# Four graph layers on one core: pieces for the first adjacency, another queue for the weights, sums as a row, a last graph without collecting DMAs, and another planned order

## The chip, the cores and the metric

The kernel runs on one core of one Trainium2 chip, in fp32. The time is device microseconds of that core for one launch, as the median of several runs.

## What is computed

For each of 32 graphs of 512 nodes with 256 features there are four layers, each followed by a residual and a layer norm:

```python
x = layernorm(x + relu(((1 + eps) * x + adj @ x) @ W1 + b1) @ W2 + b2)  # 256 -> 512 -> 256
h = x @ W                                            # 4 heads of 64
e = where(adj > 0.5, leaky_relu(e_dst[i] + e_src[j], 0.2), -1e9)
x = layernorm(x + softmax(e) @ h + bias)             # each head
q, k, v = x @ Wq.T, x @ Wk.T, x @ Wv.T               # 8 heads of 32
s = q @ k.T / sqrt(32) + log(adj + 1e-6)
x = layernorm(x + (softmax(s) @ v) @ Wo.T + bo)
s = where(nodemask, adj * ((x @ W3) @ x.T), -1e30)
x = layernorm(x + softmax(s) @ x)
```

In the code the layers count from 0 to 3.

## The kernel before

**A plan sets the order.** `fast_path` does not write its instructions in order. It registers *steps* (`step(name, engine, us, after, take, free, mode)`), each with its engine, an assumed cost, the steps it comes after and the buffers that it takes and frees. `Plan.order` then runs a list scheduler over the steps of all graphs: among the steps that can start soonest it takes the one with the smallest due time, which is the graph's number times a period, less the longest path left, plus a random displacement of the step's name, plus a weight times the price of changing PE's form of matmul (`CHANGE`). `Plan.run` tries a few sets of parameters, keeps the one with the shortest planned end and emits the instructions in that order. Each engine works through its own in order, so the plan sets the order on every engine and on every queue of DMA issues. Several graphs are under way at a time, up to six (`live`), with 14 large buffers (`B`), 13 middle ones (`C`) and the 8 PSUM banks (`p`).

**Forms of matmul.** TensorE (PE) works in four forms, which the steps name by `mode`: the full array (""), four row tiles for layer 2's scores ("row", `32*128` in the profile), four column tiles of 32 for its values and weight sums ("c32", `128*32`), and two of 64 for layer 1's output ("c64", `128*64`).

**Set-up.** `prepare` loads the weights through `load` (L314 to 320, issue at L320), all on ScalarE's DMA queue: eps, w1 with b1, w2, three bias rows, wg with a0 and a1, rawq to rawo, w3. It transposes the layer-2 weights on PE (L341) and works out bounds (`gg`, L472; `fmt`, L493); a general path exists for inputs beyond them.

**One graph.** SyncE's queue (SP) loads x (L614) and then the adjacency A (L619), 0.5 and 1 MB.
- Layer 0: 16 PE transposes of A (`AT_t`, L639), copied by ScalarE to `AT` (L647); `hT_ps` = x times AT (L671); `h1T_ps` (L694), ScalarE's relu (L700); `y_ps` (L713). The layer norm takes DVE sums, a power on GpSimd (L577) and ScalarE's scaling (L590).
- Layer 1: transposes of x (ScalarE copies them and sums each row into `xs`); values `v1`; their logits. `R`, the exponentials of one side, is transposed on PE (`R_t`, L799), written to DRAM (`R_dram`) and read back to all partitions (`R_bc`), both on SP, L809 and 811. ScalarE and DVE build the weights z (L850, L861); `o_ps` (L884). Rows without an edge need a tiny share of the sum of all values: `hs` (step `hs`, L822) is that sum, Wg applied to `xs`, and `hse` (L830) scales it; `oe` adds it to the output as a per-partition bias.
- In layers 1 and 2 the softmax denominators are column sums of large weight tiles. Accumulating DMAs on GpSimd's queue add halves of the tiles together (L912 in layer 1, L1079 in layer 2: `collect`, steps `cd` and `cs`); PE then multiplies by ones (`d_ps`, step `d2` for layer 2, L1128), and DVE takes the reciprocal (L1143).
- Layer 2: transposes of x (`xT_t`, L990), q (`qT_ps`, L1009), k and v2; scores `s` (L1046), ScalarE's exp (L1059), DVE's product with adj (L1068), values (L1104), and the output projection `o2p_ps` (L1176) after DVE's product `yT` (L1147).
- Layer 3: A is loaded again; `iT_ps` (L1215), scores (L1229), ScalarE's exp (L1257), transposes (`eT_t`, L1274), output (L1301), and the store.

Of the kernel before, what the change touches and what calls it, by code (L numbers as in the profile page):

```python
# [30 lines left out]
def row_bcast(ap, n):  # L31

    return bass.AP(tensor=ap.tensor, offset=ap.offset, ap=[[0, P], [1, n]])
# [13 lines left out]
class Plan:  # L47
# [9 lines left out]
    BACK = {"act": 0.13, "dve": 0.12}  # L57

    CHANGE = {
# [4 lines left out]
    }  # L64
# [66 lines left out]
            t = max(t, ends[h][n] + self.hop(self.steps[h][n], s))  # L131
        return t

    def order(self, period, ahead, window, stay, shift=0.0, seed=0):
# [10 lines left out]
        rng = random.Random(seed)  # L145
        moved = {n: rng.uniform(-shift, shift) for n in [*self.steps[0], *self.steps[-1]]}

        def open_to(n):
            nonlocal opened
            while opened < min(n, len(self.steps)):  # L150
                for name in self.steps[opened]:
                    if not waits[opened][name]:
                        ready[opened, name] = self.ready(opened, name, ends)
                opened += 1

        open_to(window)
        while low < len(self.steps):
            found = []
            for (g, name), t in ready.items():
                s = self.steps[g][name]  # L160
                t = max(t, engine.get(s.eng, 0.0))
                change = self.CHANGE[mode][s.mode] if s.eng == "pe" else 0.0
                for k, (kind, _, rest) in enumerate(s.take):
                    r, n = room[kind], sum(b[0] == kind for b in s.take[:k])
                    if len(r) <= rest + n:
                        break
                    t = max(t, r[n][0])
                else:
                    due = max(g - 1, 0) * period - self.left[g][name] + moved[name] + stay * change
# [47 lines left out]
def fast_path(  # L217
# [77 lines left out]
    def prev(name, i):  # L295

        return (f"{name}{i-1}",) if i else ()
# [5 lines left out]
    def prepare():  # L303
# [7 lines left out]
        def bank(key, shape):  # L311
            return ps.tile(shape, F32, tag=f"p{slot[key]}", name=key)

        def load(name, us, *transfers, take=()):  # L314


            @step(f"ld_{name}", "act", 0.5 * len(transfers), take=take)
            def _():
                for transfer in transfers:
                    nc.scalar.dma_start(*transfer())  # L320

            @step(name, "q3", us, (f"ld_{name}",))
            def _():
                pass
# [25 lines left out]
            def _():  # L350
                nc.scalar.copy(wT[name].rearrange("p c f -> p (c f)"), t[f"wt{name}"])

        load("eps", 2.0, lambda: (eps_bc, row_bcast(eps0, 1)))
# [7 lines left out]
        load(  # L361
            "w1", 3.0, lambda: (w1_sb, rows(w1)), lambda: (b1_sb, b1.rearrange("(c p) -> p c", p=P))
        )
        load("w2", 2.5, lambda: (w2_sb, rows(w2)))

        def bias_rows(k, b):
# [5 lines left out]
        load("bias", 3.0, *(bias_rows(k, b) for k, b in enumerate((b2, gbias, bo))))  # L372

        def vector(name, a):
            def transfer():
# [2 lines left out]

            return transfer

        load(
            "wg", 3.0,
            lambda: (wg_sb[:, :, :D], wg.rearrange("(c p) h f -> p c (h f)", p=P)),
            vector("a0", a_src), vector("a1", a_dst), take=("C=a0", "C=a1"),
        )

        @step("wa", "dve", 3.2, ("wg",), take=("C=prod",), free=("prod", "a0", "a1"))
# [135 lines left out]
    def graph(g):  # L523
        plan.graph()
        slot = plan.slot[-1]
        t = {"g": g}

        def big(key, shape, name):
# [88 lines left out]
        def _():  # L617
            t["A"] = big("A0", [P, NC, N], "A")
            nc.sync.dma_start(t["A"], adj[g].rearrange("(c p) m -> p c m", p=P))  # L619

        @step("ld", "q0", 8.0, ("ldA",))
# [61 lines left out]
        for f in range(HC):  # L683

            @step(
                f"f{f}", "pe", 1.72, row("he", DC) + prev("f", f) + ("^w1",),
                take=(f"p=f{f}",) + (() if f else ("B=h1T/2",)),
            )
            def _(f=f):
# [124 lines left out]
        def _():  # L814
            pass

        @step("hs", "pe", 0.9, row("xe1", DC) + ("^wa",), take=("p=hs",))
        def _():
            ph = t["phs"] = bank("hs", [P, DC], "hs_ps")
            for o in range(DC):  # L820
                for d in range(DC):
                    nc.tensor.matmul(  # L822
                        ph[:, o : o + 1], wg_sb[:, d, blk(o)], t["xs"][:, d : d + 1],
                        start=(d == 0), stop=(d == DC - 1),
                    )

        @step("hse", "act", 0.1, ("hs",), free=("hs",))
        def _():
            t["hs"] = little([P, DC], "hs")
            nc.scalar.mul(t["hs"], t["phs"], TINY)  # L830

        for c in range(NC):

# [35 lines left out]
        for hp in range(H1 // 2):  # L869
            for k in range(2):  # L870
# [221 lines left out]
        def attend(k):  # L1092
# [14 lines left out]
                        start=(c == 0), stop=(c == NC - 1),  # L1107
                    )

            if c % 2:  # L1110
                collect(k, k - 1, (f"n{k-1}", f"m{k}1"))
            if c < NC - 1:
                return
# [5 lines left out]
                nc.scalar.copy(t["yT2"][:, o, :], t[f"n{o}"])  # L1119

            a = NC * o
            collect(a + 2, a, (f"cs{a+1}", f"cs{a+3}", f"n{a+2}"))

            @step(f"d2{o}", "pe", 0.87, (f"cs{a+2}",), take=(f"p=d2{o}",), free=(f"E{a}", f"zs{a}"), mode="c32")
            def _():
                t[f"d{o}"] = bank(f"d2{o}", [P, N], f"d2_ps_{o}")
                for j in range(4):
                    nc.tensor.matmul(  # L1128
                        t[f"d{o}"][32 * j : 32 * j + 32, :], ones[:, :32], t[f"E{a}"][:, j, :],
                        start=True, stop=True,  # L1130
                    )

            @step(f"nd{o}", "act", 0.49, (f"d2{o}",), take=(f"rdT=rdT{o}",), free=(f"d2{o}",))
            def _():
# [677 lines left out]
```

## Time and profile before

| | us |
|---|---|
| median of 3 runs (range) | 3014.66 (3010.17 to 3021.8) |
| profiled execution, time | 3013.04 |
| profiled execution, span | 3011.3 |
| PE busy | 2944.1 (98%) |
| DVE busy | 2009.7 (67%) |
| ScalarE (ACT) busy | 1946.5 (65%) |
| GpSimd (POOL) busy | 619.8 (21%) |
| mean granted TensorE clock | 0.991 of full speed |

The busy time of PE comes from ends that are modelled, so lengths on PE are read from start to start. Most fp32 matmuls leave two records in the trace, so eight records are four matmuls. In a line of the timeline stand the start, the length of the group, the engine, the source line, what it writes and reads, the count, and in brackets how long the engine was idle before it and what released it. A window's line has its length, then busy time and count for each engine, the granted clock, the share of DMA and its rate. A wait's line has the total, the number of times and the longest.

### The profile page before, as it was taken

How to read it: one execution, taken by the hardware profiler on the slowest of the kernel's cores; microseconds unless marked ns; L12 is line 12 of the kernel's file. 1: busy time of each engine (PE TensorE's matmuls, PEld its weight loads, DVE VectorE, ACT ScalarE, POOL GpSimd, SP SyncE). 2: the span in 40 equal slices, each digit the busy share in tenths (PEclk: the TensorE clock that was granted, in tenths of full speed). 3: DMA queues.
4: the chain of work that ended last, by engine and by line, in shares of the span. 5: the costliest groups of instructions: out<-in, count | busy, mean ns of one | idle time of the engine just before them, and what ended most of it. 6: DMA issues, size and time to landing. Idle time of an engine off the chain costs nothing. (4 is left out here: it accounts for less than half of the span.)

```text
span 3011.3 us, 40812 instructions
## 1 busy us (share of the span) xinstructions
PE 2944.1 (98%) x15053; PEld 1703.7 (57%) x15053; DVE 2009.7 (67%) x3935; ACT 1946.5 (65%) x3849; POOL 619.8 (21%) x686
## 2 busy tenths in 40 slices
PE   7899999999999999999999999999999999999996
PEld 5544655555565555565555565555565555565544
DVE  1467576676676676676676676676676676676874
ACT  2667566767666767666767666767666767666762
POOL 0222122112222112222112222112222112222210
PEclk9999999999999999999999999999999999999998
DMA  4579767788887788887787887787877787887963
GB/s 152 125 173 194 154 137 172 160 180 177 180 168 165 161 182 174 180 166 170 160 184 171 181 166 168 160 187 168 180 163 173 160 189 168 177 168 150 199 133 79
DMA packets 159782, 500.82 MB, mean 166 GB/s; under 512 B 13132, under 2 KB 48728, under 8 KB 130904
## 3 DMA queue, kind: packets, MB, share of 16 engines
q0 software_dynamic: 78336, 352.36, 62.0%
q1 hardware_dynamic: 77824, 142.88, 13.8%
q10 hardware_dynamic: 3416, 2.90, 0.3%
q8 instruction: 121, 1.98, 0.3%
q14 instruction: 85, 0.70, 0.1%
HBM read 179.06 MB, written 17.05 MB: 65 GB/s over the span
## 5 line engine op out<-in xcount | busy, mean ns | idle before, releaser
L1068 DVE SCALAR_TENSOR_TENSOR z<-AT,z 128x1024 f32<-128x1024 f32 x512 | 610.9, 1217 | 273.2 <-ACT z L1059 272.7
L1059 ACT ACTIVATE z<-s 128x512 f32<-128x512 f32 x1024 | 551.3, 611 | 268.3 <-PE s L1046 268.1
L1143 DVE RECIPROCAL rdT<-rdT 128x256 f32<-128x256 f32 x128 | 218.3, 1728 | 316.2 <-ACT rdT L1136 316.2
L861 DVE SCALAR_TENSOR_TENSOR z<-z,T,edge 128x512 f32<-128x512 f32 x512 | 357.8, 747 | 62.2 <-ACT z L850 62.0
L850 ACT ACTIVATE z<-R_bc,nT,S 128x512 f32<-128x512 f32 x512 | 382.1, 819 | 17.8 <-DMA R_bc<-R_dram 17.8
L1079 POOL DMA_DIRECT2D z<-z x192 | 169.5, 883 | 992.2 <-PE o_ps L1104 268.7
L590 ACT ACTIVATE x<-x,shift,rstd 128x256 f32<-128x256 f32 x512 | 295.4, 602 | 108.0 <-DVE shift L582 108.0
L912 POOL DMA_DIRECT2D z<-z x256 | 228.8, 1033 | 467.5 <-DMA z<-z 265.2
L1046 PE MATMUL s<-qT,kT 32*128 32x512 f32 x2048 | 291.8, 634 | 0.1
L577 POOL TENSOR_TENSOR rstd<-ve,nhalf 128x4 f32<-128x4 f32 x128 | 134.7, 1052 | 696.9 <-DVE ve L572 671.6
L1104 PE MATMUL o_ps<-z,v 128*32 128x512 f32 x2048 | 260.5, 601 | 0.3 <-ACT z L1059 0.3
L694 PE MATMUL h1T_ps<-hT,w_sb 128*128 128x512 f32 x512 | 240.0, 604 | 0.0
L1229 PE MATMUL s<-xT,iT 128*128 128x512 f32 x512 | 237.4, 598 | 0.0
L1301 PE MATMUL o_ps<-x,eT 128*128 128x256 f32 x1024 | 237.4, 385 | 0.0
L713 PE MATMUL y_ps<-w_sb,h1T 128*128 128x256 f32 x1024 | 232.4, 381 | 2.2 <-ACT h1T L700 2.2
L884 PE MATMUL o_ps<-z,v 128*64 128x512 f32 x1024 | 230.8, 602 | 1.5 <-DVE z L861 1.5
L1301 PEld LDWEIGHTS o_ps<-x,eT 128*128 128x128 f32 x1024 | 189.5, 190 | 68.1 <-issue 22.8
L713 PEld LDWEIGHTS y_ps<-w_sb,h1T 128*128 128x128 f32 x1024 | 194.6, 191 | 52.8 <-issue 20.7
L671 PE MATMUL hT_ps<-AT,x 128*128 128x384 f32 (+2 forms) x768 | 210.1, 383 | 8.8 <-ACT AT L647 8.8
L559 DVE BATCH_NORM_STATS2 st<-x 128x6 f32<-128x256 f32 x512 | 211.9, 414 | 5.6
L1046 PEld LDWEIGHTS s<-qT,kT 32*128 32x128 f32 x2048 | 93.5, 183 | 158.7 <-issue 66.8
L694 PEld LDWEIGHTS h1T_ps<-hT,w_sb 128*128 128x128 f32 x512 | 90.5, 190 | 122.0 <-issue 112.8
(145 smaller groups left out, 4261.5 us busy)
## 6 DMA issues: line engine op xcount, KB each, us to landing
z<-z POOLq DMA_DIRECT2D x192, 1024.0 KB, 8.2
A<-in_adj_dram SPq DMA_DIRECT2D x64, 1024.0 KB, 11.0
z<-z POOLq DMA_DIRECT2D x128, 512.0 KB, 8.0
x<-biases POOLq DMA_DIRECT2D x96, 512.0 KB, 9.6
R_bc<-R_dram SPq DMA_DIRECT2D x32, 1024.0 KB, 4.5
z<-z POOLq DMA_DIRECT2D x128, 256.0 KB, 7.7
x<-in_x_dram SPq DMA_DIRECT2D x32, 512.0 KB, 6.0
out_dram<-x SPq DMA_DIRECT2D x32, 512.0 KB, 3.8
```

The costliest lines, as they stand in the source:

```text
L590: nc.scalar.activation(t["x"][:, c, :], t["x"][:, c, :], AF.Identity, bias=t["shift"][:, c : c + 1], scale=t["rstd"][:, c : c + 1],)
L694: nc.tensor.matmul(ph, w1_sb[:, d, blk(f)], t["hT"][:, d, :], start=(d == 0), stop=(d == DC - 1))
L713: nc.tensor.matmul(py[:, j, :], t["h1T"][:, f, blk(2 * c2 + j)], w2_sb[:, f, :], start=(f == 0), stop=(f == HC - 1),)
L850: nc.scalar.activation(t[f"e{h}"][:, c, :], t["Rbc"][:, h, :], AF.Relu, bias=t["nT"][:, h, c : c + 1], scale=t["S"][:, h, c : c + 1],)
L861: nc.vector.scalar_tensor_tensor(z, z, t["T"][:, h, c : c + 1], t["edge"][:, c, :], op0=ALU.add, op1=ALU.mult)
L884: nc.tensor.matmul(po[j * F1 : (j + 1) * F1, :], t["v"][:, c, h * F1 : (h + 1) * F1], t[f"e{h}"][:, c, :], start=(c == 0), stop=(c == NC - 1),
L1046: nc.tensor.matmul(pk, t["k"][hs, o, blk(c)], t["q"][hs, o, :], start=True, stop=True)
L1059: nc.scalar.activation(t[f"E{k}"][:, j, :], t[f"ps{k}{j}"], AF.Exp, scale=QSCALE)
L1068: nc.vector.scalar_tensor_tensor(z, t["AT"][:, c, None, :].to_broadcast([P, 2, N]), ADJ_EPS, z, op0=ALU.add, op1=ALU.mult,)
L1104: nc.tensor.matmul(t[f"n{o}"][32 * j : 32 * j + 32, :], t["v2"][:, c, o * P + F2 * j : o * P + F2 * (j + 1)], t[f"E{k}"][:, j, :], start=( ...
L1229: nc.tensor.matmul(pt, t["iT"][:, d, blk(c)], t["xT3"][:, d, :], start=(d == 0), stop=(d == DC - 1),)
L1301: nc.tensor.matmul(py[:, j, :], t["eT"][:, m, blk(2 * c2 + j)], t["x"][:, m, :], start=(m == 0), stop=(m == NC - 1),)
```

## The change

The diff, cut to its core. It has six parts.

1. `CHANGE` prices the way from the full array to row tiles at 0.13 instead of 0.1, and back at 0.17 instead of 0.13.
2. `order` takes a list of (seed, size) pairs instead of one; each displaces a random 15% of the step names, and the displacements add up. One set of parameters with 14 such pairs takes the place of three.
3. `load` issues on SP. The small loads (eps, b1, the bias rows, a0 and a1) stay on ScalarE's queue, b1 apart from w1 and a0 and a1 apart from wg.
4. A is loaded ahead of x, for graph 0 in four pieces of columns, and the transposes of graph 0 wait for one piece each; `h` waits for x.
5. `hs` swaps weights and moving data: a row of 256 sums instead of two columns. The row goes to DRAM and back (on SP) to stand on the partitions; `oe` waits for that.
6. For the last graph nothing is collected by DMA; `d2` multiplies all four chunks of weights by ones and adds in PSUM.

```diff
-        "": {"": 0.0, "row": 0.1, "c32": 0.1, "c64": 0.1},
-        "row": {"": 0.13, "row": 0.1, "c32": 0.2, "c64": 0.2},
+        "": {"": 0.0, "row": 0.13, "c32": 0.1, "c64": 0.1},
+        "row": {"": 0.17, "row": 0.1, "c32": 0.2, "c64": 0.2},
...
-        moved = {n: rng.uniform(-shift, shift) for n in [*self.steps[0], *self.steps[-1]]}
+        moved = dict.fromkeys((n for steps in self.steps for n in steps), 0.0)
+        for seed, far in shifts:
+            rng = random.Random(seed)
+            for n in moved:
+                if rng.random() < 0.15:
+                    moved[n] += rng.uniform(-far, far)
...
-        def load(name, us, *transfers, take=()):
+        def load(name, us, *transfers, take=(), little=False):
-            @step(f"ld_{name}", "act", 0.5 * len(transfers), take=take)
+            @step(f"ld_{name}", "act" if little else "sp", 0.5 * len(transfers), take=take)
             def _():
                 for transfer in transfers:
-                    nc.scalar.dma_start(*transfer())
+                    (nc.scalar if little else nc.sync).dma_start(*transfer())
...
-        @step("ldx", "sp", 0.1, take=("live", "C=x/2"))
-        @step("ldA", "sp", 0.1, ("ldx",), take=("L0", "B=A0/5"))
+        pieces = NC if g == 0 else 1
+        for m in range(pieces):
+            @step(f"lp{m}", "sp", 0.4 if g == 0 else 0.1, prev("lp", m), ...)
+            def _(m=m):
+                cols = slice(m * N // pieces, (m + 1) * N // pieces)
+                nc.sync.dma_start(
+                    t["A"][:, :, cols], adj[g].rearrange("(c p) m -> p c m", p=P)[:, :, cols]
+                )
+        @step("ldx", "sp", 0.1, (f"lp{pieces-1}",), take=("C=x/2",))
...
-                f"at{m}", "pe", 0.44, ("ld",) + prev("at", m),
+                f"at{m}", "pe", 0.44, (f"la{m if g == 0 else 0}",) + prev("at", m),
-                f"h{d}", "pe", 3.49, row("ate", NC) + row("atd", NC) + prev("h", d),
+                f"h{d}", "pe", 3.49, row("ate", NC) + row("atd", NC) + prev("h", d) + ("lx",),
...
-            for o in range(DC):
-                for d in range(DC):
-                    nc.tensor.matmul(
-                        ph[:, o : o + 1], wg_sb[:, d, blk(o)], t["xs"][:, d : d + 1],
-                        start=(d == 0), stop=(d == DC - 1),
-                    )
+            for d in range(DC):
+                nc.tensor.matmul(
+                    ph[:1, :], t["xs"][:, d : d + 1], wg_sb[:, d, :D],
+                    start=(d == 0), stop=(d == DC - 1),
+                )
+            nc.scalar.mul(t["hsr"], t["phs"][:1, :], TINY)
+        @step("hsd", "sp", 0.1, ("hse",))
+        def _():
+            nc.sync.dma_start(hs_dram, t["hsr"])
+            nc.sync.dma_start(t["hs"], hs_dram.rearrange("o (c p) -> p (o c)", p=P))
...
-                f"oe{hp}", "act", 0.59, (f"o1{hp}1", "hse") + prev("oe", hp),
+                f"oe{hp}", "act", 0.59, (f"o1{hp}1", "hsl") + prev("oe", hp),
...
-            if c % 2:
+            if c % 2 and not last:
                 collect(k, k - 1, (f"n{k-1}", f"m{k}1"))
...
-            @step(f"d2{o}", "pe", 0.87, (f"cs{a+2}",), take=(f"p=d2{o}",), free=(f"E{a}", f"zs{a}"), mode="c32")
+            chunks = range(a, a + NC) if last else (a,)
+            @step(f"d2{o}", "pe", 0.87 * len(chunks), ..., mode="c32")
+                for b in chunks:
+                    for j in range(4):
+                        nc.tensor.matmul(
+                            t[f"d{o}"][32 * j : 32 * j + 32, :], ones[:, :32], t[f"E{b}"][:, j, :],
+                            start=(b == a), stop=(b == chunks[-1]),
+                        )
...
-        plan.run([(28, 0.0, 6, 100.0, 8.0, 34035), (28, 0.05, 6, 30.0, 3.0, 427523), (28, 0.0, 6, 15.0)])
+        plan.run([(26, 0.05, 6, 40.0, ((364910, 5.0), (601245, 5.0), (535451, 2.0), (139611, 2.0), (551513, 5.0), (226, 10.0), (156506, 2.0), (365686, 2.0), (878334, 2.0), (617633, 2.0), (623088, 5.0), (5628, 5.0), (102860, 2.0), (997287, 2.0)))])
```

More of the change, by code (lines that the diff above doesn't have):

```diff
@@ L132, in ready, with order @@
         return t
-    def order(self, period, ahead, window, stay, shift=0.0, seed=0):
+    def order(self, period, ahead, window, stay, shifts=()):
         room = {b: [(0.0, i) for i in range(n)] for b, n in self.stock.items()}
@@ L144, in order @@
         todo = [len(steps) for steps in self.steps]
-        rng = random.Random(seed)
-        moved = {n: rng.uniform(-shift, shift) for n in [*self.steps[0], *self.steps[-1]]}
+        moved = dict.fromkeys((n for steps in self.steps for n in steps), 0.0)
[4 more added lines that the diff above has]
+                    moved[n] += rng.uniform(-far, far)
         def open_to(n):
@@ L351, in _ @@
                 nc.scalar.copy(wT[name].rearrange("p c f -> p (c f)"), t[f"wt{name}"])
-        load("eps", 2.0, lambda: (eps_bc, row_bcast(eps0, 1)))
+        load("eps", 2.0, lambda: (eps_bc, row_bcast(eps0, 1)), little=True)
         @step("selfw", "dve", 0.5, ("eps",))
@@ L359, in _ @@
             nc.vector.tensor_scalar_mul(selfw, ident, eps1)
-        load(
-            "w1", 3.0, lambda: (w1_sb, rows(w1)), lambda: (b1_sb, b1.rearrange("(c p) -> p c", p=P))
-        )
+        load("b1", 2.0, lambda: (b1_sb, b1.rearrange("(c p) -> p c", p=P)), little=True)
+        load("w1", 2.5, lambda: (w1_sb, rows(w1)))
         load("w2", 2.5, lambda: (w2_sb, rows(w2)))
@@ L370, in bias_rows @@
             )
-        load("bias", 3.0, *(bias_rows(k, b) for k, b in enumerate((b2, gbias, bo))))
+        load("bias", 3.0, *(bias_rows(k, b) for k, b in enumerate((b2, gbias, bo))), little=True)
         def vector(name, a):
@@ L379, in vector @@
             return transfer
[L381 to L387, printed above, removed]
+        load("a", 2.0, vector("a0", a_src), vector("a1", a_dst), take=("C=a0", "C=a1"), little=True)
+        load("wg", 2.0, lambda: (wg_sb[:, :, :D], wg.rearrange("(c p) h f -> p c (h f)", p=P)))
+        @step("wa", "dve", 3.2, ("wg", "a"), take=("C=prod",), free=("prod", "a0", "a1"))
         def _():
@@ L525, in graph @@
         slot = plan.slot[-1]
+        last = g == B - 1
         t = {"g": g}
@@ L609, in _ @@
                     norm_stats(n, c)
-        @step("ldx", "sp", 0.1, take=("live", "C=x/2"))
+        pieces = NC if g == 0 else 1
+        for m in range(pieces):
+            @step(
+                f"lp{m}", "sp", 0.4 if g == 0 else 0.1, prev("lp", m),
+                take=() if m else ("live", "L0", "B=A0/5"),
+            )
+            def _(m=m):
+                if m == 0:
+                    t["A"] = big("A0", [P, NC, N], "A")
+                cols = slice(m * N // pieces, (m + 1) * N // pieces)
+                nc.sync.dma_start(
+                    t["A"][:, :, cols], adj[g].rearrange("(c p) m -> p c m", p=P)[:, :, cols]
+                )
+            @step(f"la{m}", "q0", 8.0 if g else 1.5 if m else 3.5, (f"lp{m}",))
+            def _():
+                pass
+        @step("ldx", "sp", 0.1, (f"lp{pieces-1}",), take=("C=x/2",))
         def _():
@@ L614, in _ @@
             nc.sync.dma_start(t["x"], x[g].rearrange("(c p) d -> p c d", p=P))
-        @step("ldA", "sp", 0.1, ("ldx",), take=("L0", "B=A0/5"))
[L617 to L621, printed above, removed]
+        @step("lx", None, 5.0, ("ldx",))
         def _():
@@ L685, in _ @@
             @step(
-                f"f{f}", "pe", 1.72, row("he", DC) + prev("f", f) + ("^w1",),
+                f"f{f}", "pe", 1.72, row("he", DC) + prev("f", f) + ("^w1", "^b1"),
                 take=(f"p=f{f}",) + (() if f else ("B=h1T/2",)),
@@ L815, in _ @@
             pass
-        @step("hs", "pe", 0.9, row("xe1", DC) + ("^wa",), take=("p=hs",))
+        @step("hs", "pe", 0.43, row("xe1", DC) + ("^wa",), take=("p=hs",))
         def _():
-            ph = t["phs"] = bank("hs", [P, DC], "hs_ps")
-            for o in range(DC):
-                for d in range(DC):
-                    nc.tensor.matmul(
-                        ph[:, o : o + 1], wg_sb[:, d, blk(o)], t["xs"][:, d : d + 1],
-                        start=(d == 0), stop=(d == DC - 1),
-                    )
-        @step("hse", "act", 0.1, ("hs",), free=("hs",))
-        def _():
+            ph = t["phs"] = bank("hs", [P, D], "hs_ps")
+            for d in range(DC):
[3 more added lines that the diff above has]
+                )
+        @step("hse", "act", 0.3, ("hs",), free=("hs",))
+        def _():
+            t["hsr"] = small.tile([1, D], F32, tag="hsr", name=f"hsr_{g}", bufs=1)
+            nc.scalar.mul(t["hsr"], t["phs"][:1, :], TINY)
+        @step("hsd", "sp", 0.1, ("hse",))
+        def _():
+            hs_dram = dram.tile([1, D], F32, tag="hs_dram", name=f"hs_dram_{g}")
+            nc.sync.dma_start(hs_dram, t["hsr"])
             t["hs"] = little([P, DC], "hs")
-            nc.scalar.mul(t["hs"], t["phs"], TINY)
+            nc.sync.dma_start(t["hs"], hs_dram.rearrange("o (c p) -> p (o c)", p=P))
+        @step("hsl", None, 6.0, ("hsd",))
+        def _():
+            pass
         for c in range(NC):
@@ L1121, in attend @@
             a = NC * o
-            collect(a + 2, a, (f"cs{a+1}", f"cs{a+3}", f"n{a+2}"))
-            @step(f"d2{o}", "pe", 0.87, (f"cs{a+2}",), take=(f"p=d2{o}",), free=(f"E{a}", f"zs{a}"), mode="c32")
+            chunks = range(a, a + NC) if last else (a,)
+            if not last:
+                collect(a + 2, a, (f"cs{a+1}", f"cs{a+3}", f"n{a+2}"))
+            @step(
+                f"d2{o}", "pe", 0.87 * len(chunks),
+                tuple(f"m{b}1" for b in chunks) if last else (f"cs{a+2}",), take=(f"p=d2{o}",), mode="c32",
+            )
             def _():
                 t[f"d{o}"] = bank(f"d2{o}", [P, N], f"d2_ps_{o}")
[L1127 to L1131, printed above, removed]
+                for b in chunks:
[3 more added lines that the diff above has]
+                            start=(b == a), stop=(b == chunks[-1]),
+                        )
+            for b in chunks:
+                for key in (f"E{b}", f"zs{b}"):
+                    plan.free(key, (f"d2{o}", f"n{b}"))
             @step(f"nd{o}", "act", 0.49, (f"d2{o}",), take=(f"rdT=rdT{o}",), free=(f"d2{o}",))
```

## The prediction

> **What bounds the kernel now.** I read the slices first, then waits, windows and the chain, then single runs on TensorE (PE).
>
> ```profile
> PE   7899999999999999999999999999999999999996
> PEclk9999999999999999999999999999999999999998
> ```
>
> PE is full and at full clock but for three slices at the head and one at the end. The windows (length, then busy us of PE, PEld, DVE, ACT, POOL; clock; DMA) say how full:
>
> ```profile
> 0.00:40.00 40.00, 19.57 (x79) 14.10 (x80) 5.35 (x20) 7.55 (x12) 2.02 (x11) 1.00 0.71 230
> 80.00:140.00 60.00, 50.55 (x225) 30.28 (x224) 33.79 (x80) 38.08 (x71) 14.18 (x16) 0.91 0.55 116
> 200.00:220.00 20.00, 15.22 (x43) 8.53 (x44) 11.67 (x21) 14.84 (x24) 4.36 (x4) 0.74 0.56 136
> 480.00:2840.00 2360.00, 2360.00 (x12224) 1367.11 (x12224) 1635.90 (x3186) 1584.52 (x3138) 502.91 (x551) 1.00 0.79 172
> 2940.00:2999.00 59.00, 46.12 (x170) 28.78 (x169) 27.86 (x60) 18.29 (x38) 2.91 (x3) 0.88 0.30 77
> ```
>
> From 480 to 2840 us PE never pauses: there only less PE work shortens the kernel. The same layer-1 matmul recurs 181.06 us apart two graphs on (950.36 and 1131.42 in the timeline), so a graph is 90.5 us of PE, 32 are 2896, some 2903 with the set-up. The last matmul ends at 2998.7; what is missing, 95 us, is idle or slow-clock time: about 60 ahead of 480, about 33 after 2840, where PE waited for this:
>
> ```profile
> PE AT_t L639 <- DMA A<-in_adj_dram: 11.6, 1, 11.6
> PE hT_ps L671 <- ACT AT L647: 8.8, 1, 8.8
> PE qT_ps L1009 <- ACT xT L994: 5.2, 2, 4.8
> PE fmt L493 <- DVE fmax L488: 4.8, 1, 4.8
> 2934.05 12.76 DMA z<-z
> 2947.34 10.10 DMA z<-z
> 2964.08 6.06 PE L1176 MATMUL o2p_ps<-woT,yT 128*128 128x256 f32 x14 [4.81 <-DVE yT L1147]
> ```
>
> The last three lines are the end of the chain and its timeline: two accumulating DMAs one after the other, then PE waits 4.81 us for what they feed. And the price of changing PE's form of matmul, in the timeline:
>
> ```profile
> 1085.93 1.98 PE L694 MATMUL h1T_ps<-hT,w_sb 128*128 128x512 f32 x4
> 1087.85 1.14 PE L1046 MATMUL s<-qT,kT 32*128 32x512 f32 x8
> 1088.92 0.28 PE L799 MATMUL R_t<-ident,R 128*16 128x128 f32 x1
> 1089.03 3.60 PE L694 MATMUL h1T_ps<-hT,w_sb 128*128 128x512 f32 x8
> 1092.56 1.07 PE L1104 MATMUL o_ps<-z,v 128*32 128x512 f32 x8
> 1093.56 1.14 PE L1046 MATMUL s<-qT,kT 32*128 32x512 f32 x8
> ```
>
> Records of 512 columns inside a run stand 0.429 apart, so eight four-abreast s records are 0.857; from start to start they took 1.07, 0.21 more. The c32 run (L1104) took 1.00, 0.14 more; the full-array run of four took 1.92 for 1.72, 0.20 more. The single R_t among full-array work took 0.11, its bare length.
>
> **The skill.** "TensorEngine Tiling (Array Packing)", Key Properties, says that a change of tiling mode drains the array; the trace agrees, at 0.14 to 0.21 us a run. "TensorE: Matmul & The Clock Gate", What's actually happening, lets an idle window of about 3.4 us halve the clock; the trace agrees: 0.74 granted in 200:220, about the 4.8 us wait of fmt. "DMA: Bandwidth & Descriptors", Issuing engines are not separate DMA queues, says that another issuing engine saves only issue time; the head below is worked out so. "ScalarE: Activation LUTs", What ACT_TABLE_LOAD costs, gives about 1283 ns; the trace has 1.28.
>
> **Part by part.**
>
> *Row of value sums (hs).* Before: 4 matmuls, 8 records, 949.48 to 950.36 = 0.88 us. After: 2 matmuls, 4 records of 256 columns; such records stand 0.216 apart (v_ps, eight in 1.73), so 0.86. Gain 0.02 × 32 = **1 us**. The trace has no one-column weights that stream 256: if a record pair took half, 0.43 a graph, the gain is 14; if its narrow tile drained the array at 0.2 to 0.3, a loss of 6 to 10. R_t, as narrow, paid nothing, so I take 1. The copy of the row on ScalarE (0.19 before, some 0.3) and two DMAs on SP stay hidden: the round trip R_dram then R_bc landed in 1.4 + 4.5 us, and in the new order at least 65 us of PE work (the sum of record distances in the changed list) lie between hs and the first reader in the steady state. The issues (about 0.5 us each) stand on SP ahead of later loads. Without that cover the readers, oe on ScalarE, would stop ScalarE for some 8 us.
>
> *Order and switch prices.* I counted runs of one form in both instruction lists. Before: 265 full, 222 row, 175 c32, 36 c64, 698 in all; after: 198, 251, 131, 71, 651. At 0.19 (a full run with what follows), 0.21, 0.14 and 0.16 (c64: a 32-record run took 7.02 for 32 × 0.2145) that is 127 and 120: **−7 us**. The steps themselves are the same, and steps that only move among each other on PE cost nothing while it is never idle: what hides them is PE's own 90.5 us a graph against 62.7 of DVE and 60.8 of ACT (its 1635.90 and 1584.52 over 26.08 graphs). A run's price differs with its neighbours; 0 to −12.
>
> *Last graph.* Six 1 MB accumulating DMAs go. d2 becomes 32 records instead of 8, twice: 24 × 2 × 0.107 = **+5 us** on PE. For it go: the 12.76 and 10.10 us at the end of the chain and d_ps's waits (3.3 in all). d2 of both halves now stands well ahead; between the second and o2p lie 6.6 us of PE work against a chain of 0.59 (ACT), 3.37 and 0.61 (DVE) = 4.6, so the 4.81 wait goes. 3.4 us of layer-3 work now lie between o2p and the next transposes, which waited 4.11: about 1 stays. The next to be late are the exponentials and products of the last layer-2 group, 1 to 3 us. With the clock nearer to full, the tail's 33 us of loss becomes about 14 (8 to 22): **−19**.
>
> *Start.* The first adjacency landed at 11.47 and x, 0.5 MB, at 7.2. Four pieces of 256 KB ahead of x (three more issues, 0.5 us each on SP) let the transposes begin at about 5, the first hT at about 12.5 instead of 24.5: 7 small loads stay on ScalarE in place of 16, and ScalarE's copies no longer stand behind loads (8.8 us). SP takes the weights over, and its queue is waited on too: in the changed list piece 3 waits for eps, x for b1's landing, the weights each for an earlier load. But graph 1's adjacency is now behind all of it: about 5.25 MB; 6.5 MB had landed by 26.3 before, 0.28 MB/us after the first 3, so it lands at about 22 (20 to 26). Before, its transposes began at 33.2. The stretch of PE work ahead of it is the same, so I count the start at **−10.5** (−12.5 to −7.5).
>
> *Fill, 40 to 480.* Loss about 36. In the new order fmt and its like stand behind 95 to 220 us of PE work, so 4.8 + 2.5 go; the transposes of x before layer 2 have 13 us of work to cover a chain of 14.4 where 120:140 lost 8.3; at 200:220 half stays, because hs's DMAs stand ahead of R's on SP. A new wait is near graph 2's first q. I take 22: **−13** (−20 to −6).
>
> Sum: −1 −7 +5 −19 −10.5 −13 = −45.5. The profiled execution is 3013.04 for a span of 3011.3; it becomes 2966 in span, 2967.5 in time. The median of the runs stands 1.6 over the profiled one: about **2970**.
>
> **Rivals.**
>
> *The row is cheap.* At 0.43 a graph: 14 less, **2956**. For it: fewer instructions. Against: every 256-column pair in the trace takes 0.43 per matmul, and there are two of them.
>
> *The head gains little.* Graph 1's adjacency at 30 and the fill as before: 22 more, **2990**. For it: SP now carries 3 MB of weights, waits for landings, and hs. Against: 0.28 MB/us was sustained with both queues.
>
> *The change does not do what it says.* Runs are fewer but no cheaper, and hs pays a switch of 0.3: 7 + 10 more, **2987**. R_t speaks against it.
>
> *Slower: the steady state gets waits.* Now PE loses nothing in 2360 us. In the new order the cover between producer and consumer shrinks: h1T's last copy to y from 7.8 us of PE work to 1.7, k to s from 15.1 to 1.9, layer 3's transposes down to 1.7, i to s down to 1.3; the ACT copy needed takes 0.6 to 0.7, but with one z of 0.61 (L1059) or a product of 1.2 (L1068) queued ahead, some 2 us. R_t to the first layer-1 output falls from 42.8 to 27.9, and on SP hs's DMAs, waiting for ScalarE, hold R's back. From 45.5 / 32 = 1.4 us a graph it decides: at 2 us it is **3034**. Against: ACT is 67% and DVE 69% busy there, and with several graphs under way all the waits of the steady state are nil today.
>
> **How the numbers follow.** 0.5%, 15 us, is about what a measurement of this kernel tells from no change. Chances: forecast 0.60 (its own range 2955 to 2985), cheap row 0.12, weak head 0.14, no savings 0.06, steady waits 0.08. The first two are faster; the next two mostly, since 2990 and 2987 are under 3000 with some spread: 0.84 faster, 0.08 within, 0.08 slower. The range reaches from the cheap row with a good tail, 2940, to the weak head with the unknown switches, 3002.
>
> **What would show it.** Right: PE full between 480 and 2840 but with graphs 0.2 to 0.3 us shorter; hs runs of 0.86; first hT near 12 and graph 1's AT_t near 22; no DMA z<-z in the chain's last 60 us; no wait over 3 us at o2p. Wrong: waits of PE on ACT or DVE in the steady state (a PE busy below 2355 there), graph 1's AT_t waiting past 26, hs off 0.86, or R_bc named ahead of z with ScalarE idle.

## The result: a tenth slower, in every graph of the steady state

The changed kernel takes 3342.87 us (3338.76 to 3346.06, 4 runs), the kernel before 3012.41 beside it: a ratio of 1.1091, interval 1.106 to 1.1121. The profiled execution has a span of 3338.3 against 3011.3, 327 us more. The prediction was 2970.

The slices and the windows of the changed kernel (length, busy us of PE, PEld, DVE, ACT, POOL, clock, DMA):

```profile
PE   9988999898898988989989898898988989989977
0.00:40.00 40.00, 32.25 (x146) 24.07 (x147) 9.91 (x35) 10.57 (x17) 2.70 (x12) 1.00 0.67 204
80.00:140.00 60.00, 60.00 (x299) 37.08 (x301) 28.72 (x66) 40.02 (x83) 15.72 (x17) 1.00 0.83 166
200.00:220.00 20.00, 20.00 (x134) 8.52 (x133) 18.47 (x30) 14.42 (x30) 5.57 (x6) 1.00 0.95 175
480.00:2840.00 2360.00, 2170.88 (x10594) 1214.61 (x10587) 1429.79 (x2767) 1371.73 (x2722) 435.50 (x476) 0.95 0.68 150
```

The first slices are fuller than before, as forecast; but PE, which never paused between 480 and 2840 us, now is idle for 189 us of them, and its granted clock falls to 0.95. Its waits:

```profile
PE qT_ps L1036 <- ACT xT L1021: 117.0, 26, 11.1
PE d_ps L957 <- issue: 52.4, 15, 4.3
PE d_ps L957 <- DMA z<-z: 34.6, 10, 4.0
PE s L1266 <- ACT iT L1258: 21.9, 22, 7.2
PE o2p_ps L1213 <- DVE yT L1184: 8.5, 1, 8.5
```

The first four are paid in nearly every graph: for layer 2's transposed x, for layer 1's weight sums (GpSimd's adds), for `iT`. Where the second line has "issue", the trace names nobody; in the graph at 1115 the last packets of layer 1's adds end at 1115.29, 0.42 us ahead of `d_ps`. Take the start of `R_t` as each graph's mark. The first comes 16 us earlier than before (52.6 for 68.7); from graph 0 to 5 another 3 are gained; from 5 to 28 it takes 2393.3 instead of 2085.0; from 28 to 31, 294.7 instead of 262.9; from there to the end 217.1 instead of 211.1. −16.1 − 3.0 + 308.3 + 31.8 + 6.0 = 327. Between graphs 12 and 20 one takes 104.1 us instead of 90.5. Most of the 308 is accounted for by the window from 480 to 2840: 189 us of idle time, and about 113 for the slow clock (the clock of the trace has a mean of 0.952 there, and 0.048 of 2360 is 113, an estimate).

What PE waits for at qT is told by the chain of waits in one such graph (start, length, what):

```profile
1052.93 10.05 DMA R_dram<-R_rows
1063.12 4.58 DMA R_bc<-R_dram
1067.81 0.18 ACT z L877
...
1073.24 5.03 ACT z L877 x7
1078.27 0.48 ACT xT L1021
1078.79 3.78 PE qT_ps L1036 x4
```

The write of R, 8 KB, took 10.05 us; before, 1.4 in the median. ScalarE meanwhile stands at its first z of layer 1 (184 us of waiting for R_bc in all), and layer 2's copies of xT are queued behind fourteen of these z, and the copy of iT behind three, so that PE's waits for iT come from R too. PE waits for xT, and then runs four records of q in 3.78 us instead of 1.72, at the slow clock. The timelines of SP's and GpSimd's queues in the same graph show what R_dram stood among:

```profile
1050.82 0.92 POOL L1106 DMA_DIRECT2D z<-z  x1
1052.12 0.87 POOL L547 DMA_DIRECT2D x<-biases  x1 [0.39 <-PE R_t L815]
1052.50 0.38 SPq L1367 DMA_DIRECT2D out_dram<-x  x1
1052.93 1.32 SPq L825 DMA_DIRECT2D R_dram<-R_rows  x1
1063.12 0.34 SPq L827 DMA_DIRECT2D R_bc<-R_dram  x1
```

The store of a finished graph, 0.5 MB, is issued 0.43 us ahead of it on the same queue, and GpSimd has an add of 1 MB under way (one of layer 2's, L1106; those that `d_ps` waits for are layer 1's, L939). In the kernel before the store stood 7.5 us ahead of R_dram (1082.06 and 1089.54 in its timeline), and no add was issued in the 4.9 us on either side. The trace's DMA packets say the same: the add's 8 KB packets, 0.75 us each in the mean, ran from 1052.3 to 1058.4, the bias's to 1061.5; the store's last of 512 small packets ended at 1062.39, and R_dram's sixteen ran from 1062.12 to 1062.42. From graph 8 to 29, R_dram's last packet ended 9.4 to 10.7 us after its issue in every one.

### The profile page after: what moved, and what is told of

Read it like the earlier page. It is cut to its first block, busy times and chain, and to the rows that moved or that the text cites. A ratio compares the mean times of both kernels' runs of the same rounds, so it can differ in the third digit from the quotient of the medians.

```text
span 3338.3 us, 40913 instructions
## 1 busy us (share of the span) xinstructions
PE 3066.6 (92%) x14973; PEld 1708.6 (51%) x14973; DVE 2026.7 (61%) x3935; ACT 1945.1 (58%) x3849; POOL 618.7 (19%) x680
## 3 DMA queue, kind: packets, MB, share of 16 engines
q1 hardware_dynamic: 90608, 145.57, 12.6%
## 4 chain that ended last, share of the span: by engine, by line
PE 63%; DMA 15%; ACT 12%; DVE 5%; issue 3%; SPq 0%; POOL 0%; ACTq 0%; POOLq 0%
PE s L1073 8%; DMA R_dram<-R_rows 8%; ACT z L877 7%; PE o_ps L911 7%; PE o_ps L1338 7%; PE o_ps L1131 6%; PE qT_ps L1036 4%; DMA R_bc<-R_dram 4%; PE kT_ps L1036 4%; PE s L1266 4%; PE o2p_ps L1213 3%; PE v_ps L776 3%; DMA z<-z 3%; PE v_ps L1054 3%; ACT x L591 2%
## 5 line engine op out<-in xcount | busy, mean ns | idle before, releaser
L1095 DVE SCALAR_TENSOR_TENSOR z<-AT,z 128x1024 f32<-128x1024 f32 x512 | 617.8, 1218 | 414.0 <-ACT z L1086 413.7
L1086 ACT ACTIVATE z<-s 128x512 f32<-128x512 f32 x1024 | 566.1, 604 | 325.7 <-PE s L1073 257.5
L591 ACT ACTIVATE x<-x,shift,rstd 128x256 f32<-128x256 f32 x512 | 279.9, 594 | 91.8 <-DVE shift L583 91.6
L1106 POOL DMA_DIRECT2D z<-z x186 | 164.7, 931 | 831.7 <-PE o_ps L1131 500.5
L1073 PE MATMUL s<-qT,kT 32*128 32x512 f32 x2048 | 304.3, 665 | 3.3 <-ACT kT L1042 3.3
L578 POOL TENSOR_TENSOR rstd<-ve,nhalf 128x4 f32<-128x4 f32 x128 | 143.8, 1124 | 849.3 <-DVE ve L573 848.1
L939 POOL DMA_DIRECT2D z<-z x256 | 236.7, 1058 | 345.4 <-DMA z<-z 193.0
L1131 PE MATMUL o_ps<-z,v 128*32 128x512 f32 x2048 | 271.1, 632 | 0.0
L1036 PE MATMUL qT_ps<-xT,wqT 128*128 128x512 f32 x256 | 161.8, 765 | 117.1 <-ACT xT L1021 117.0
L1266 PE MATMUL s<-xT,iT 128*128 128x512 f32 x512 | 243.8, 605 | 22.0 <-ACT iT L1258 21.9
L911 PE MATMUL o_ps<-z,v 128*64 128x512 f32 x1024 | 238.9, 603 | 5.1 <-DVE z L888 4.9
L710 PE MATMUL h1T_ps<-hT,w_sb 128*128 128x512 f32 x512 | 227.3, 593 | 0.0
L547 POOL DMA_DIRECT2D x<-biases x96 | 85.0, 893 | 668.1 <-issue 420.8
```

What stands on the lines that cost most here:

```text
L591: nc.scalar.activation(t["x"][:, c, :], t["x"][:, c, :], AF.Identity, bias=t["shift"][:, c : c + 1], scale=t["rstd"][:, c : c + 1],)
L911: nc.tensor.matmul(po[j * F1 : (j + 1) * F1, :], t["v"][:, c, h * F1 : (h + 1) * F1], t[f"e{h}"][:, c, :], start=(c == 0), stop=(c == NC - 1),
L1036: nc.tensor.matmul(pq, wT[n][:, d, blk(o)], t["xT2"][:, d, :], start=(d == 0), stop=(d == DC - 1))
L1073: nc.tensor.matmul(pk, t["k"][hs, o, blk(c)], t["q"][hs, o, :], start=True, stop=True)
L1086: nc.scalar.activation(t[f"E{k}"][:, j, :], t[f"ps{k}{j}"], AF.Exp, scale=QSCALE)
L1095: nc.vector.scalar_tensor_tensor(z, t["AT"][:, c, None, :].to_broadcast([P, 2, N]), ADJ_EPS, z, op0=ALU.add, op1=ALU.mult,)
```

## Experiments

Three theories were set against one another. Cover is the work on PE that lies between a producer and the step that reads from it. **Theory 1**: two transfers last longer than the new order leaves room for. One is R's round trip, which stands behind the store; the other is the adds of layer 1. **Theory 2**: the new order leaves too little cover in many places, so that mending one only moves the wait. **Theory 3**: the read-back of hs in four-byte pieces clogs SP's queue. All kernels but the last keep the order of steps as it was, but for the moves named.

### The store behind R

```diff
 # in run(), on the ordered list: where SP's next step after a store is R's
+            if sp and seq[sp[0]][1] == "Rd":
+                seq.insert(sp[0], seq.pop(k))     # "out" goes behind "Rd"
```

> The changed kernel, its order kept but for one move: on SP's queue the store of a finished graph (out_dram), which stood directly ahead of R_dram, goes directly behind R_bc. Theory 1 (R is queued behind the 0.5 MB store, which GpSimd's accumulating DMAs starve: R_dram lands 9.5 us after its issue in 24 steady graphs against 1.0 before): R_dram lands within 2.5 us, about 8 us a graph come back, 24 x 8 = 190, time 3130 to 3170; PE's waits for qT (117 us in all) vanish, those for d_ps of layer 1 (87 us) stay. Theory 2 (the new order leaves too little cover in many places, R is one of them): the wait moves to the next tight producer, time 3280 or more. Theory 3 (the 256 four-byte pieces of the read-back of hs, some 6 us ahead of R_dram on the same queue, clog it): R_dram still lands 6 us or more after its issue, time as the changed kernel, 3343.

Measured: 3249.61 us, 93 fewer than the changed kernel (ratio to before 1.0781, 1.0763 to 1.0799). Half of what theory 1 gave, because R_dram is still not quick (the chain of this run):

```profile
1138.25 6.66 DMA R_dram<-R_rows
1145.04 5.95 DMA R_bc<-R_dram
```

With the store away its packets end 5.1 us after the issue instead of 9.5; GpSimd's add is still issued 1.5 us ahead of it, and its packets ran until 1144.55. The waits for d_ps stay as they were (52.0 and 34.2), those for qT fall from 117.0 to 77.6 and those for iT from 21.9 to 7.8.

### hs in columns, in the changed kernel's order

```diff
-                    ph[:1, :], t["xs"][:, d : d + 1], wg_sb[:, d, :D],
+                        ph[:, o : o + 1], wg_sb[:, d, blk(o)], t["xs"][:, d : d + 1],
...
-            nc.sync.dma_start(hs_dram, t["hsr"])
-            nc.sync.dma_start(t["hs"], hs_dram.rearrange("o (c p) -> p (o c)", p=P))
```

> The changed kernel, its order kept, but hs computed as before: four matmuls to two columns, scaled by ScalarE, no DMA to DRAM and back. Theory 1 (the store ahead of R): R_dram still stands behind the store, time 3325 to 3350. Theory 3 (the four-byte read-back clogs SP's queue): R_dram lands in 2 us, time 3150 or less. If the narrow row tile of the new hs drained the array at each visit, 6 to 10 us fewer than the changed kernel, if it is as dear as before, 0 to 2.

Measured: 3319.42, 23 fewer, and 6 below the range of theory 1. In the steady state nothing changes: 104.1 us a graph, R_dram's last packet still 9.3 to 10.6 after its issue from graph 8 to 29. Theory 3 falls for the steady state. What the row costs lies in the first graphs, up to the mark of graph 5 (433.2 with the row, 414.2 without). The waits of SP's queue in the changed kernel between 140 and 260 us name it:

```profile
SPq L851 <- ACT hsr L846: 81.9, 2, 56.8
SPq L827 <- DMA R_dram<-R_rows: 10.8, 2, 7.0
SPq L853 <- DMA hs_dram<-hsr: 7.4, 2, 4.8
```

SP stands before the write of a later graph's hs, and R_dram of graph 2, whose rows were ready at 155.98, is issued at 168.78 (157.05 without hs's DMAs).

### The row alone, in the order before

The same edit the other way round, in the kernel before.

> The kernel before in its own order, with hs alone as in the change (row, DRAM, back; the two DMAs issued on SP where ScalarE's scaling of hs stood). Theory 1 and 2 (the parts do little, the order does it): 3002 to 3015. Theory 3 (the read-back clogs SP's queue): R_dram of this kernel lands late too where hs stands ahead of it, 3050 or more.

Measured: 3038.13, 1.0075 of the kernel before (1.0053 to 1.0096); outside what any theory gave. The row costs 23 to 25 us in either order. The profiled execution is 26.7 longer than the one before; by the marks 19.5 of them are lost up to graph 5, where ScalarE waits for the read-back, as the list of who waits for hs says:

```profile
  DMA hs<-hs_dram: 37.3, 6
```

Of the rest 2.3 lie between the marks of graphs 5 and 31, where a steady graph takes 90.69 instead of 90.53, and 5.0 after the mark of graph 31; why these last are lost was not shown. In the changed kernel's timeline the row's four records take 0.96 from start to start; the columns took 0.88.

```profile
1043.61 1.02 PE L838 MATMUL hs_ps<-wg_sb,xs 128*1 128x256 f32 x4
1044.57 0.49 PE L687 MATMUL hT_ps<-ATd,x 128*128 128x128 f32 x2
```

### All parts in the order before

```diff
-                    nc.scalar.dma_start(*transfer())
+                    (nc.scalar if i in small_ones else nc.sync).dma_start(*transfer())
...
+        seq.insert(a, seq.pop(b))                 # graph 0: "ldA" (in four pieces) ahead of "ldx"
...
+                chunks = range(a, a + NC) if g == B - 1 else (a,)
```

with the row as above.

> The kernel before in its own order, with the parts 3 to 6 of the change put in (weights on SP, the first adjacency ahead of x in pieces, hs as a row, the last graph's weight sums on PE), the steps otherwise in the places that they had. Theory 1 and 2 (the loss of the change is in its order): head 10 to 20 us shorter, tail 10 to 20 us shorter, steady state as before, 2975 to 2995. Theory 3: 3050 or more, from hs.

Measured: 3042.42 (1.0093, 1.0076 to 1.011), in neither of the two ranges. A steady graph takes 90.69, as with the row alone: no part of the change is what makes the steady state slow; its order is. But head and tail brought nothing here.

### R ahead of the add

On top of the store behind R:

```diff
+            if names[k - 1][1] == "h1":           # PE's step ahead of R_t
+                for name in ("Rt", "Re", "Rd"):
+                    move((g, name), names[k - 1][:2])
```

> The run with the store behind R_bc, and in addition R_t goes between the two halves of the next graph's hT on PE instead of behind both (3.5 us of PE work earlier), with R_rows and R_dram along, so that R_dram is issued ahead of GpSimd's 1 MB add and not 0.1 to 1.5 us after it. Theory 1 (R's round trip is late because its small packets share the DMA engines with that add and with the store): R_dram lands within 2 us of its issue, ScalarE's first z of layer 1 starts 6 us or more earlier, PE's waits for qT (78 us in that run) and the slow clock after them go, 80 to 110 us: 3140 to 3170. Theory 2 (little cover in many places): PE waits elsewhere instead, 3210 or more.

Measured: 3153.95 (1.0475, 1.0458 to 1.0493), 96 fewer than the run before it, as theory 1 said. R_dram is issued 1.2 us ahead of the add and lands 1.0 after its issue; the first z of layer 1 starts 11.5 after the issue, where it took 12.8 in the run before this one and 14.9 in the changed kernel; ScalarE's waits for R_bc fall from 125.9 to 37.5. R_dram was also issued earlier, by the 3.5 us of PE work over which R_t moved, so the run doesn't tell how much of the 96 us comes from the way past the add and how much from the earlier start. The waits for qT are 14.9 in all, 10.9 of them in one of the first graphs. Those for d_ps stay:

```profile
PE d_ps L974 <- issue: 53.7, 15, 5.7
PE d_ps L974 <- DMA z<-z: 33.9, 10, 3.8
PE qT_ps L1053 <- ACT xT L1038: 14.9, 5, 10.9
```

So of the 9.5 us that R_dram took, 4.4 went with the store and then 4.1 with the add; 1.0 is its own. The store beside no add was not tried.

### Layer 1's weight sums later

```diff
+            if [s[1] for s in names[k + 1 : k + 5]] == ["n3", "s5", "o111", "o101"]:
+                later((g, "d1"), names[k + 4][:2])   # d1 and what needs it go behind o101
```

> The same, and layer 1's weight sums (d1, line d_ps) go some 5.5 us later on PE, behind the layer-2 values, scores and layer-1 output that followed them. PE waited 86 us there for GpSimd's adds. Theory 1 (two transfers that take longer than the plan assumes, R and these adds, are all that the new order loses): another 90 to 120 us, 3030 to 3070, and no wait of PE over 1 us between 600 and 2800. Theory 2: at most 40 us more, 3110 or more, with new waits.

Measured: 3079.15 (1.0215, 1.0198 to 1.0232): 75 fewer. The waits for d_ps are gone (2.4 in all); a new one comes, 21.0 at the scores behind it, 0.9 in each of 24 graphs. Between the theories: most of the wait was removed, and a piece of it moved.

### The same with hs in columns

> The same, with hs in columns and no DMA. By the run with columns alone (23 us less than the changed kernel) and that with the row alone in the order before (25 us more): 20 to 28 us less than the run without this edit, whichever theory holds; of these 0.17 us a graph, 5, on PE and the rest in the first four graphs, where the read-back is waited for.

Measured: 3043.29, 36 fewer, more than the row cost in the other two pairs and than the 20 to 28 expected: 19.5 up to the mark of graph 5, as there, and 13.9 from there to graph 28, which were not traced further. The timeline shows the new wait:

```profile
1128.88 1.07 PE L987 MATMUL d_ps<-z,ones 128*32 128x512 f32 x8
1130.84 2.09 PE L1103 MATMUL s<-qT,kT 32*128 32x512 f32 x8 [0.89 <-ACT dT L998]
1132.86 1.99 PE L1243 MATMUL o2p_ps<-woT,yT 128*128 128x256 f32 x8
```

The scores read nothing of dT; what ties them to it is the PSUM bank that d_ps holds. They wait 0.89 for ScalarE's copy of d_ps, and then take 2.02 for their usual 1.07; why so long was not shown. It is a mark that the experiment itself made.

### Head and tail alone

The kernel before with parts 3, 4 and 6, in its own order.

> The kernel before in its own order, with parts 3, 4 and 6 (weights on SP, first adjacency in pieces ahead of x, last graph's weight sums on PE), hs as before. If only the row made the run of all parts slow: 3042 - 25 = 3017, so that head and tail bring nothing without an order that uses them; if they bring the 10 to 20 us each that I counted: 2975 to 2995.

Measured: 3016.15, ratio 1.0013 (1.0006 to 1.002), as the first of the two expectations said. The mark of graph 5 comes 0.7 us earlier than before, that of graph 31 3.5 earlier; the 2.8 between them are about what the profiled execution before lost in one wait (2.2 at y_ps) with the slow clock after it. From the mark of graph 31 to the end it takes 216.6 instead of 211.1. The 5.5 more are the PE work of the longer d2, which I had put at 5; the six DMAs that went save nothing, since d2 and o2p stand where they stood and the waits of 4.8 (o2p) and 4.1 (xT_t) with them.

### Weight sums less late

```diff
-                later((g, "d1"), names[k + 4][:2])
+                later((g, "d1"), names[k + 3][:2])   # between o111 and o101
```

> The run with R early, d1 late and hs in columns, but d1 one step less late: between the two halves of layer 1's output instead of behind both, so that ScalarE's copy of it (dT, 0.7 us) lies beside 1.8 us of PE work and the scores that need its bank don't wait for it. There PE waited 0.89 and then ran a scores group of 1.07 in 2.02, 1.84 us a graph. Theory 1 (R, the adds of layer 1 and the row are all that the steady state lost): 24 x 1.84 = 44 less than 3043, 2995 to 3005. If the adds are not done by then (the transfers behind d1 end up to 1.8 us later): 3005 to 3030. Theory 2: no change, 3040.

Measured: 3001.73 (2999.18 to 3003.75, 6 runs), ratio **0.9966 (0.9954 to 0.9978)**: faster than the kernel before by 10 us. The window of the steady state, and from PE's waits of the whole run the longest and those for qT and layer 1's d_ps:

```profile
480.00:2840.00 2360.00, 2352.76 (x12176) 1353.90 (x12174) 1643.73 (x3171) 1564.75 (x3121) 495.08 (x541) 1.00 0.78 170
PE o2p_ps L1243 <- DVE yT L1214: 12.7, 1, 12.7
...
PE qT_ps L1066 <- ACT xT L1051: 6.0, 5, 2.7
...
PE d_ps L987 <- DMA z<-z: 3.3, 6, 1.9
```

PE is full again at full clock but for 7.2 us. Store, R_t, d1 and hs: with these four put right, 341 us are back. Theory 2 falls: no other place of the new order makes PE wait in the steady state. But that is all the new order does there. By the marks the whole gain is in the head: 35.5 us are gained up to graph 5; from there to graph 28 it takes 2097.5, 12.5 more than before, and from there to the end 13.8 more.

### A new plan with longer transfers

```diff
-        @step("Rl", None, 8.5, ("Rd",))
+        @step("Rl", None, 11.0, ("Rd",))
-                @step(f"as{h}{k}", None, 2.5, (f"aq{h}{k}",))
+                @step(f"as{h}{k}", None, 4.0, (f"aq{h}{k}",))
...
-        plan.run([(26, 0.05, 6, 40.0, (...))])
+        plan.run([(30, 0.0, 6, 60.0, (...))])        # 19 pairs drawn anew
```

> Parts 3, 4 and 6 of the change with hs in columns (as a step of the plan), and a new order: the plan assumes 11 us for R's round trip instead of 8.5 and 4 for the landing of layer 1's adds instead of 2.5, and its displacements were drawn anew for these. R_dram is planned 7.8 us after the store and at no add's time. Theory 1 (the order was bad by these two assumed durations): steady graphs at 90.5 to 91 us without a wait for either, head and tail as in the other runs with the parts: 2975 to 3010. Theory 2 (orders annealed on assumed durations lose cover somewhere, whichever two are mended): over 3040, with other waits.

Measured: 3036.89 (1.0087, 1.0074 to 1.0101), between the two expectations. A steady graph takes 91.8. R no longer stops PE at qT, but the copy iT, which stands on ScalarE behind a z that waits for R_bc, does (the list of waits, then the chain of one graph):

```profile
PE s L1256 <- ACT iT L1248: 26.0, 18, 3.0
...
1071.46 10.50 DMA R_bc<-R_dram
...
1082.05 0.81 ACT z L867
1082.87 0.48 ACT iT L1248
...
1083.39 4.56 PE s L1256 x10
```

In graphs 7 to 12 R_dram landed 3.0 to 4.6 us after its issue and R_bc's last packets came 8.5 to 10 us after theirs (4.2 in the kernel before), with an add of layer 2 issued 2.9 us later than R_dram and that of the bias 3.3 ahead. So it is R again: the plan now assumes 11 us for the round trip, and beside these adds it took 12.6 to 15.0. PE is idle for 26 us between 480 and 2840, 1.0 of the 1.2 us by which a steady graph is longer than before. A fixed duration, even a longer one, does not hold for a transfer whose time depends on what else is under way.

## Why the prediction was wrong

**The steady state.** The step that failed stands under *Order and switch prices*: steps that only move among each other on PE cost nothing while it is never idle, because DVE's 62.7 and ScalarE's 60.8 us hide behind PE's 90.5. That compares busy times and leaves out the transfers, and it put the waits of the new order at nothing. They cost 13.6 us a graph, 308 of the 327. I gave the slower rival 0.08 and 2 us a graph. It named the right place (R_t's cover falling from 42.8 to 27.9 us of PE work), and the sign set down for it came true (R_bc ahead of z, with ScalarE idle for 184 us). But its mechanism, hs's DMAs holding R back, is not that of the steady state, and what I had under it failed in four places.

- *R's price.* I took 1.4 + 4.5 us from the row of DMA issues. That was R's time where it stood before: the store 7.5 us ahead and no add beside it. In the new place R_dram's packets take 9.5. I read the order of the queue for who waits for whom, and not for what is still being moved when a small transfer is issued. Shown by the first and the fifth experiment: 9.5, 5.1, 1.0. The trace before had a case of it. In graph 2 R_dram, issued 4.5 us behind an add, took 5.6 us to land, the longest of those that the view lists (1.3 to 5.6, 1.4 in the median), and what followed is the chain of the changed kernel:

```profile
204.24 0.81 ACT L850 ACTIVATE z<-R_bc,nT,S 128x512 f32<-128x512 f32 x1 [8.21 <-DMA R_bc<-R_dram]
204.96 0.56 ACT L994 COPY xT<-xT_t 128x512 f32<-128x512 f32 x1
205.57 3.78 PE L1009 MATMUL qT_ps<-xT,wqT 128*128 128x512 f32 x4 [4.78 <-ACT xT L994]
```

I took the slow clock of 200:220 for that of fmt's wait. But fmt stands at 130.5; the 4.8 us of 200:220 are this wait at qT.
- *Who is behind the waiting instruction.* I measured R's cover up to the first layer-1 output. The wait ended elsewhere: the z on ScalarE stand ahead of layer 2's copies of xT, and PE's q came first. Some 10 us of z lie between R_bc and that copy.
- *The adds of layer 1.* They have no line in my working. They cost 87 us of waits, some 3.5 in each of 25 cases, and the slow clock after them; moving d1 by some 3.7 us of PE work was enough.
- *"All the waits of the steady state are nil today"* was my argument against. It says how much cover the old order has, and nothing of the new.

**The slow clock** was not in the rival's price. In the graph shown the waits of 4.52 us at qT and 3.48 at d_ps were followed by matmuls at half speed: 3.78 for 1.72, with a granted clock of 0.50 from 1077.6 to 1084.3 and from 1115.1 to 1118.4. The whole steady state has 0.95.

**hs.** The term was −1. It was +23 to +25, shown in both orders: about 20 in the first graphs, a little on PE (90.69 − 90.53 a graph, where I had −0.02), and in the old order 5 at the end whose cause stays open. I had claimed a cover of 65 us for the steady state, which held, and had let it stand for the first graphs too, where graphs follow each other otherwise and SP is one queue: its wait for hs held R back by 12.8 us at graph 2. That I had priced only as a loss of some us at 200:220.

**Runs of one form.** −7 was forecast. In the mended run a steady graph takes 90.89, of which 0.28 is idle time (7.2 us in 26 graphs), and one run is added by moving d1. No saving is seen: before, it took 90.53. Why the lists' 47 fewer runs are worth nothing was not tried.

**Head.** Right in its steps, and near in size: first hT at 11.95 (12.5 forecast), graph 1's transposes at 21.41 (22), the first mark 16 us earlier; the waits of gg and fmt are gone, and 80:140 and 200:220 are full. In the mended run the mark of graph 5 comes at 416.8 instead of 452.3, 35.5 for the 23.5 that I had. In the changed kernel it came at 433.2; that the 19.1 gained look like the forecast is luck, since the row took as much again (414.2 without it). And it takes the order to use the parts: in the old order they brought 0.7 up to there.

**Tail.** −19 and +5 were forecast, +6 measured. The last graph's own waits went as forecast: no wait at its o2p (3292), and after 3240 PE waits only 7.0 us in all. But the graph before it, which still collects layer 2's weights by DMA, now waits at its o2p:

```profile
3221.75 1.07 PE L1161 MATMUL d_ps<-z,ones 128*32 128x512 f32 x8
3231.29 5.41 PE L1213 MATMUL o2p_ps<-woT,yT 128*128 128x256 f32 x16 [8.48 <-DVE yT L1184]
```

The chain that I had worked out as 4.6 us for the last graph stands there without cover, with the last graph's layer norm in between on DVE. And ScalarE waited 7.8 us for hs's read-back, which held iT back by 7.2.

## What to carry to other kernels

A small transfer on which every graph depends can be as slow as what is issued just ahead of it on its queue and what another queue moves meanwhile (here 1.0 to 9.5 us); look at the neighbours of such a transfer in the new order and at its longest case in the old, not at the median. When an order is planned on assumed durations and the shortest of many plans is kept, nothing guards the cover that those durations make look free; how the order here came to lose its cover was not tested. Check first the steps whose real time is not constant. A wait is paid where the next thing behind it on an in-order engine is needed, so follow the queue behind the waiting instruction up to PE.

## What the runs showed of the hardware

An 8 KB write from SP took 1.0 us alone, 5.1 beside a 1 MB accumulating DMA of GpSimd, and 9.5 behind a 0.5 MB store as well. The Trainium skill, "DMA: Bandwidth & Descriptors", Queues, rings and completion order, says that each DMA engine takes turns between its queues by packets, and that a packet holds several descriptors. In the run with the store away, 112 of the add's 128 pieces of 8 KB, 0.75 us each in the mean, had begun before the first of R_dram's sixteen pieces did; on 16 engines that is seven of eight. So the turns were not piece by piece. Whether the add's pieces make up one packet in the page's sense no run shows, and the 5.1 us can't be worked out from the page. A one-column weight that streams 256 columns took 0.24 a record, with what leaving it costs, more than the 0.216 of a full one.
